# Loads of x split over two queues, regrouped 1x1 stores, an earlier branch, projection in image order and two blocks of logits together

## The chip, the cores and the metric

The kernel runs on one core of a Trainium2 chip. The metric is the device time of one execution in microseconds, the lower the better. The core has five engines with an instruction queue each: TensorE (PE) for matrix products, VectorE (DVE), ScalarE (ACT) and GpSimd (POOL) for elementwise work, and SyncE (SP), which here only issues DMAs. ACT and POOL can issue DMAs too. SBUF is the working memory, PSUM the memory that TensorE writes its products to, and HBM holds the inputs, the output and scratch arrays.

## The reference

The input x has 48 channels of 256 x 256. Two layers follow each other, each a residual on a group normalisation (16 groups, no learned scale):

```python
x = x + L0(gn(x))
x = x + L1(gn(x))

def L0(x):
    qkv = einsum('bchw,oc->bohw', x, w_qkv)          # 1x1, 48 -> 144
    qkv = dwconv3x3(qkv, w_dw)                       # depthwise
    q, k, v = split(qkv, 3)                          # each unfolded in 4x4 patches, padding 4
    q, k = l2norm(q), l2norm(k)                      # 8 heads of 96 channels
    attn = softmax(einsum('bhcn,bhcm->bhnm', q, k) * temperature)
    out = fold(einsum('bhcn,bhnm->bhcm', v, attn))   # sums over n
    return einsum('bchw,oc->bohw', out, w_proj)

def L1(x):                                           # in windows of 64 x 64, 3 terms
    return einsum('bcphqw,twW,thH,tcC->bCpHqW', xb, Ws, Hs, Cs)
```

There are 4096 patches inside the image (and a border of patches of zeros, which only adds to the sums of the softmax). Each head so makes a 4096 x 4096 matrix of exponentials.

## The kernel before

The image is cut into an upper and a lower half, which lie on partitions 16 to 63 and 64 to 111 (`rows_of`), so that 96 rows of partitions hold 48 channels twice.

**Start.** Ten pieces of x (seven of 16 rows of each half, then 8, 4 and 4) are loaded into `xr`, two DMAs a piece, all on SP (L442). ACT clears the 16 unused partitions of each piece (`clear`, L120), and DVE takes statistics of it (`bn_stats`, L444). `group_stats` makes mean and inverse deviation, which are folded into the weights.

**1x1 product of heads 0 and 1.** Their 36 channels of q, k and v are computed from `xr` in 16 groups of rows (L497 to L519). TensorE writes a PSUM tile, ACT and DVE each evict half of it into one of four buffers `oi`, and four DMAs store it to the scratch `t1[0]`: for each of two column blocks of 64 partitions (`c`) and each half of the image (`s`) one DMA of 36 partitions, the upper half on SP, the lower on POOL. The other six heads' product is done later, in strips, between the blocks of the attention (class `Strip`).

**Depthwise convolution of head 0** (`depthwise_first`, L382). Rows of `t1[0]` are loaded as `pad`; half of the rows are convolved on TensorE with nine diagonal matrices `diag` (made by nine POOL products, L387), half on DVE. After the normalisation q, k and v are stored to the scratch `qkv[0]`, q and k each as a high and a low part (`oh`, `ol`).

**Branch** (L538). A block for large temperatures follows under `tc.If`: a second pass that finds the maxima of the logits. With these inputs it isn't taken. Every engine loads the flag and jumps.

**Attention** (L572 to L801). The order of all engines is written out by hand (`tc.manual_schedule`). For each head and each of 32 blocks of 128 patches, `scores` makes the logits in four steps `j` of six products (L361), each followed by an exponential on ACT that also sums (L617). `normalised` divides v by the sum; `weigh` (L651) multiplies v with the exponentials of two blocks, and DVE adds the result to `oacc` (L665). PSUM tiles `big` have three buffers, exponentials `e` three. Before it, keys of head 0 are loaded over SP, ACT and POOL. The next head's convolution, its loads and stores and the strips are spread over the blocks. Results go to the scratch `os_`.

**Projection** (L803 to L902). The output of the attention is read back in eight parts, as `pot` tiles of 16 planes (one for each place in a 4 x 4 patch). The first part was loaded into four freed key tiles (`kt`). For each row `ki` of the patch, `project` multiplies with the weights into a PSUM tile that is ordered by plane (L818), and DVE adds it to x with a reading and writing order that steps by four pixels (L825); statistics for the second layer follow (L827), and POOL stores the result to `x1s` (L830). SP loads `pot` (L889) and x (L894); ACT clears the unused partitions of the tiles (L868 to L870).

**Layer 1** (L930 to L1083) contracts over channels, width and height on TensorE and is not touched.

Of the kernel before, what the change touches and what calls it, by code (L numbers as in the profile page):

```python
# [9 lines left out]
F32 = mybir.dt.float32  # L10
F32R = mybir.dt.float32r
AF = mybir.ActivationFunctionType
# [6 lines left out]
H = W = 256  # L19
HALF = H // 2  # L20
P2 = 2 * C
OFF = 16
# [27 lines left out]
def conv_preact_kernel(  # L50
# [114 lines left out]
    def both_halves(t, y, n, base=0):  # L165

        return [t[:, base + s * HALF + y : base + s * HALF + y + n, :] for s in range(2)]
# [9 lines left out]
    class Strip:  # L177
# [5 lines left out]
        def load(self):  # L183
            self.xs = xss[self.j % len(xss)]
            for s, rows in enumerate(both_halves(xc, SR * self.j, SR)):
                nc.sync.dma_start(out=self.xs[rows_of[s]], in_=rows)
# [21 lines left out]
        def store(self):  # L208
            for s, rows in enumerate(both_halves(t1[1], SR * self.j, SR, base=1)):
                nc.sync.dma_start(out=rows, in_=self.ot[:, s])  # L210
# [171 lines left out]
    def depthwise_first():  # L382

        with tc.tile_pool(name="dg", bufs=1) as dg, tc.tile_pool(name="dps", bufs=3, space=PSUM) as dps:
            diag = dg.tile([NP1, 9, NP1], F32, name="diag")
            for t in range(9):
                nc.gpsimd.tensor_scalar_mul(diag[:, t, :], ident[:NP1, :NP1], dwt[:, 0, t : t + 1])  # L387
# [3 lines left out]
            def taps(r):  # L391
# [12 lines left out]
            with tc.manual_schedule(engines={mybir.EngineType.PE}):  # L404
                taps(0)
                for i in range(0, CR + 1, 2):
                    if i + 1 not in on_tensor:
                        taps(i + 1)
                    taps(min(i + 2, CR))
# [17 lines left out]
    with tc.tile_pool(name="xn", bufs=1) as xnp, tc.tile_pool(name="cst", bufs=1) as cst, tc.tile_pool(  # L427
        name="nps", bufs=2, space=PSUM
# [64 lines left out]
        ois = [xnp.tile([128, 2, OR, W + 2], F32, name=f"oi{i}") for i in range(4)]  # L493
# [3 lines left out]
        for n in range(QR // OR):  # L497
# [32 lines left out]
    for t in ots:  # L530
        nc.gpsimd.memset(t[:, :, :, 0:1], 0.0)
        nc.gpsimd.memset(t[:, :, :, W + 1 : W + 2], 0.0)
    xss = [cv.tile([PF, SR, W], F32, name=f"xs{i}") for i in range(2)]
    for t in xss:
        nc.gpsimd.memset(t[:OFF], 0.0)
    depthwise_first()

    with tc.If(nc.values_load(large) > 0):  # L538
        with tc.tile_pool(name="sps", bufs=2, space=PSUM) as sps:
            for j in range(HALF // SR):  # L540
                w = Strip(j)
                w.load()
                w.run(sps)
                w.store()
        for h in range(1, NH):
            depthwise_all(h)
        with tc.tile_pool(name="mk", bufs=NM) as mk, tc.tile_pool(name="mq", bufs=2) as mq, tc.tile_pool(
            name="mps", bufs=2, space=PSUM
        ) as mps:
            for h in range(NH):  # L550
# [5 lines left out]
                for nb in range(NB):  # L556
# [13 lines left out]
                    nc.vector.tensor_reduce(nmx[:, b : b + 1], mx, AX.X, ALU.max, negate=True)  # L570

    with tc.tile_pool(name="ahead", bufs=2) as ah, tc.tile_pool(name="ae", bufs=3) as ae, tc.tile_pool(  # L572
# [34 lines left out]
        def scores(h, nb, behind=None):  # L607

            b = h * NB + nb
            e = ae.tile([128, NT], F32, name="e")  # L610
            zs = asm.tile([128, 5], F32, name="zs")
            nc.scalar.activation(zs[:, 4:5], nmx[:, b : b + 1], AF.Exp, bias=border)
            kts = [keys[h, m] for m in range(NM)]
            for j in range(4):
                ps = big.tile([128, 2, 512], F32, name="big")
                logits(ps, queries[h, nb // 2], kts, nb % 2 * 128, j)
                nc.scalar.activation(  # L617
                    e[:, j * 1024 : (j + 1) * 1024],
                    ps.rearrange("p a b -> p (a b)"),
                    AF.Exp,  # L620
                    bias=nmx[:, b : b + 1],
                    accum_out=zs[:, j : j + 1],
                )
                if j == 0 and behind:
                    behind()
            return h, nb, e, zs
# [73 lines left out]
        strips[0].load()  # L700
        with tc.manual_schedule():
            load_query(0, 1)
            block = scores(0, 0)
            for h in range(NH):
                more = h + 1 < NH
                rows = {r: Depthwise(h + 1, r) for r in range(CR + 1)} if more else {}
                for g in range(NG):
# [25 lines left out]
                    block = scores(h, g * G + 1, p and p.norm)  # L733
# [14 lines left out]
                    second = block  # L748
                    if g + 1 < NG:
                        block = scores(h, (g + 1) * G)  # L750
                    elif more:
                        block = scores(h + 1, 0)
                    blocks.append(normalised(*second))
# [22 lines left out]
                    for k in range(NK):  # L776
# [18 lines left out]
                        if not more and 0 < g <= 2 * NX and k in (1, 3):  # L795
                            i = (g - 1) * 2 + k // 2
                            t, y = i // 4, i % 4 * (RP // 4)
                            for half, src in enumerate(both_parts(xc, t, y, RP // 4)):
                                nc.sync.dma_start(out=xts[t][rows_of[half], y : y + RP // 4, :], in_=src)
# [9 lines left out]
        def project(k, pot, part, xt, new):  # L809

            R = xt.shape[1]
            n = R // KS * PX
            xv = xt.rearrange("p (py ki) (px kj) -> p ki kj py px", ki=KS, kj=KS)
            for ki in range(KS):
                ps = new(n)
                step = 512 // n
                for i in range(0, KS, step):
                    nc.tensor.matmul(  # L818
                        ps[:, i : i + step, :],
                        lhsT=wp,  # L820
                        rhs=pot(ki)[:PF, i : i + step, part * n : (part + 1) * n],
                        start=True,
                        stop=True,
                    )
                nc.vector.tensor_add(xv[:, ki], ps.rearrange("p k (py px) -> p k py px", py=R // KS), xv[:, ki])  # L825
# [3 lines left out]
            for half, rows in enumerate(both_parts(x1s, k, part * R, R)):  # L829
                nc.gpsimd.dma_start(out=rows, in_=xt[rows_of[half]])  # L830

        def in_big(n):

            ps = big.tile([128, 2, 512], F32, name="big")
            return ps[:PF].rearrange("p a (b n) -> p (a b) n", n=n)
# [26 lines left out]
    with tc.tile_pool(name="pj", bufs=1) as pj, tc.tile_pool(name="pjs", bufs=1) as pjs, tc.tile_pool(  # L862
# [3 lines left out]
        pxts = [pj.tile([PF, r, W], F32, name=f"pxt{t}") for t, r in enumerate((RP, RP, PR))]  # L866
# [19 lines left out]
        for k, xus_k in enumerate(xus, 1):  # L886
# [3 lines left out]
            if k >= NX:  # L890
                for part, xt in enumerate(xus_k):
                    R = xt.shape[1]
                    for s, rows in enumerate(both_parts(xc, k, part * R, R)):
                        nc.sync.dma_start(out=xt[rows_of[s]], in_=rows)  # L894
            for part, xt in enumerate(xus_k):
# [5 lines left out]
                    lambda n: pps.tile([PF, KS, n], F32, name="pps"),  # L901
# [223 lines left out]
```

## Time and profile before

| | us |
|---|---|
| runs: median of 3 (lowest to highest) | 3571.19 (3565.88 to 3576.49) |
| the profiled execution | 3563.74 |
| its span, first to last instruction | 3561.9 |
| TensorE busy | 3324.8 |
| granted TensorE clock, mean | 0.978 |
| exponentials on ACT (L617), 1024 times 1118 ns | 1144.6 |
| adds in the projection (L825), 1024 columns, first four | 1.98 each |
| adds of the attention (L665), 1024 columns | 1.22 each |

By time: x and its statistics until 88 us; the 1x1 product until 158; the convolution of head 0 until 281; loads of keys until 306; attention until 3188; projection and second statistics until 3324; layer 1 to the end.

In a group's row stand the line, engine and operation, output and input, how often, busy time, mean duration, and the idle time of the engine before it with what ended it. A window's row gives the busy time of each engine in a stretch, the clock granted to TensorE (1.00 is full), the share of time in which the 16 DMA engines were busy, and the bytes moved per second. The chain of waits follows the last instruction back through whatever released each step.

### The profile page before, as it was taken

To read this page: it belongs to the slowest core of one execution; us is meant where nothing else is said; L and a number is where in the kernel's file an instruction comes from. 1 tells how busy PE (TensorE), PEld (TensorE's weight loads), DVE (VectorE), ACT (ScalarE), POOL (GpSimd) and SP (SyncE) were. 2 spreads that over 40 slices of the span, in tenths; PEclk is the share of its full clock that TensorE was granted. 3 is DMA by queue.
4 is the path that set the end of the run, shared out by engine and by line. 5 is a ranking of instruction groups with operands and counts; after the bars stand their busy time and mean duration, and the time that the engine had idled before them with its cause. 6 is when DMAs were issued, how large, how long until landed. Compare 5 with 4: busy or idle time off the path is not lost.

```text
span 3561.9 us, 63455 instructions
## 1 busy us (share of the span) xinstructions
PE 3324.8 (93%) x25964; PEld 1856.3 (52%) x25964; DVE 1982.3 (56%) x2965; ACT 1953.2 (55%) x2891; POOL 588.0 (17%) x658
## 2 busy tenths in 40 slices
PE   0696999999999999999999999999999999986898
PEld 0243445555555555555555555555555555542576
DVE  4372666148825882588258826872687222228544
ACT  3234667657755665566557655764666444423243
POOL 2231111012211220122012201220122010000123
PEclk9897999999999999999999999999999999997999
DMA  9445666543332333333333332333333222109764
GB/s 147 143 127 147 164 161 165 168 137 93 86 87 79 93 87 83 89 95 82 85 87 95 79 87 83 93 89 78 87 96 93 76 53 51 33 25 295 176 163 112
DMA packets 232563, 380.22 MB, mean 107 GB/s; under 512 B 77858, under 2 KB 176546, under 8 KB 229192
## 3 DMA queue, kind: packets, MB, share of 16 engines
q1 hardware_dynamic: 192246, 262.98, 27.6%
q0 software_dynamic: 36544, 110.12, 13.7%
q8 instruction: 208, 3.41, 0.4%
q10 hardware_dynamic: 3474, 2.97, 0.3%
q14 instruction: 91, 0.75, 0.1%
HBM read 230.82 MB, written 144.90 MB: 105 GB/s over the span
## 4 chain that ended last, share of the span: by engine, by line
PE 85%; DMA 5%; DVE 1%; issue 1%; SPq 0%; ACT 0%; POOL 0%; POOLq 0%; DVEq 0%; ACTq 0%
PE big L361 39%; PE big L651 36%; PE pb L1015 2%; PE pa L991 2%; PE pc L1034 2%; DMA lxq<-in_x_dram 2%; PE big L194 2%; DMA xs<-in_x_dram 2%; PE pst L599 1%; DMA kt<-qkv 0%; PE pn L268 0%; PE pps L818 0%; DVE acc L249 0%; PE big L818 0%; DMA pad<-t 0%
## 5 line engine op out<-in xcount | busy, mean ns | idle before, releaser
L617 ACT ACTIVATE e<-big,nmx 128x1024 f32<-128x1024 f32 x1024 | 1144.6, 1118 | 909.6 <-PE big L361 883.7
L361 PE MATMUL big<-kt,qt 128*128 128x512 f32 x6144 | 1459.9, 395 | 29.7 <-DMA qt<-qkv 23.4
L651 PE MATMUL big<-e,vn 128*32 128x512 f32 x12288 | 1348.4, 593 | 1.0 <-DVE vn L635 1.0
L361 PEld LDWEIGHTS big<-kt,qt 128*128 128x128 f32 x6144 | 1143.3, 189 | 370.0 <-issue 122.0
L665 DVE TENSOR_TENSOR oacc<-big,oacc 128x1024 f32<-128x1024 f32 x359 | 438.5, 1221 | 766.9 <-PE big L651 766.9
L651 PEld LDWEIGHTS big<-e,vn 128*32 128x32 f32 x12288 | 384.5, 110 | 881.9 <-issue 815.5
L249 DVE SCALAR_TENSOR_TENSOR acc<-pad,dwt,acc 126x1024 f32<-126x1024 f32 x592 | 765.5, 1293 | 34.0 <-ACT acc L230 18.3
L319 POOL DMA_DIRECT2D qkv<-o x72 | 52.9, 734 | 1341.0 <-ACT o L303 1341.0
L313 POOL TENSOR_TENSOR ol<-o,oh 126x1024 fp32r<-126x1024 f32 x78 | 185.3, 2376 | 266.5 <-DVE ss L264 197.4
L631 DVE TENSOR_REDUCE zt<-zs 128x1 f32<-128x5 f32 x256 | 38.6, 151 | 327.6 <-ACT e L617 291.2
L617 ACT ACTIVATION_READ_ACCUMULATOR e<-big,nmx 128x1 f32 x1024 | 195.8, 191 | 0.0
L303 ACT COPY o<-acc 126x1024 f32<-126x1024 f32 x74 | 161.8, 2186 | 0.0
L1022 ACT COPY lyt<-pb 128x1024 f32<-128x1024 f32 x69 | 69.9, 1012 | 111.6 <-PE pb L1015 111.6
L201 ACT ACTIVATE ot<-big,bias 108x1024 f32<-108x1024 f32 x64 | 68.0, 1112 | 112.2 <-PE big L194 74.9
L230 ACT ACTIVATE acc<-pad,dwt 126x1024 f32<-126x1024 f32 x74 | 84.1, 1136 | 77.8 <-DMA pad<-t 69.7
L676 POOL DMA_DIRECT2D os__70<-oacc x86 | 50.3, 593 | 424.2 <-DVE oacc L665 414.4
L238 PE MATMUL dps<-pad,diag 126*126 126x512 f32 x216 | 95.6, 602 | 19.3 <-DMA pad<-t 19.3
L260 ACT ACTIVATE sq<-acc 126x1024 f32<-126x1024 f32 x74 | 78.2, 1057 | 59.6 <-DVE acc L249 48.5
L335 POOL DMA_DIRECT2D kt<-qkv x44 | 22.9, 538 | 516.6 <-PE big L361 418.9
L818 PE MATMUL pps<-pot,wp 112*112 112x512 f32 x112 | 68.9, 775 | 39.0 <-DMA pot<-os__70 20.7
L1001 DVE COPY lzt<-pa 128x864 f32<-128x864 f32 (+1 forms) x69 | 67.5, 1000 | 59.9 <-PE pa L991 59.9
L264 DVE TENSOR_REDUCE ss<-sq 126x64 f32<-126x1024 f32 x80 | 97.3, 1218 | 5.4 <-ACT sq L260 5.3
(154 smaller groups left out, 1973.4 us busy)
## 6 DMA issues: line engine op xcount, KB each, us to landing
pad<-t SPq DMA_DIRECT2D x238, 254.0 KB
t<-ot SPq DMA_DIRECT2D x64, 435.4 KB
qkv<-ol POOLq DMA_DIRECT2D x78, 336.0 KB, 6.4
qkv<-oh POOLq DMA_DIRECT2D x70, 336.0 KB, 5.7
qt<-qkv SPq DMA_DIRECT2D x176, 96.0 KB
xs<-in_x_dram SPq DMA_DIRECT2D x64, 192.0 KB
out_dram<-lrt POOLq DMA_DIRECT2D x96, 128.0 KB, 3.5
qkv<-o POOLq DMA_DIRECT2D x72, 168.0 KB, 3.4
```

The lines of the kernel that those rows point to most:

```text
L194: nc.tensor.matmul(ps[:M1, s, :], lhsT=wr[r], rhs=self.xs[r, i : i + 2, :].rearrange("p a b -> p (a b)"), start=True, stop=True,)
L230: nc.scalar.mul(self.acc, self.pad[:, 0:KS, 0:W], dwt[:, self.h, 0:1])
L238: nc.tensor.matmul(ps[:, i, :], lhsT=diag[:, tap, :], rhs=self.pad[:, y : y + 2, dx : dx + W], start=(tap == 0), stop=(tap == 8),)
L249: nc.vector.scalar_tensor_tensor(self.acc, self.pad[:, dy : dy + KS, dx : dx + W], dwt[:, self.h, tap : tap + 1], self.acc, ALU.mult, ALU.add,
L260: nc.scalar.activation(self.sq, self.acc, AF.Square)
L264: nc.vector.tensor_reduce(self.ss, self.sq.rearrange("p a (x b) -> p x a b", b=KS), AX.XY, ALU.add)
L303: nc.scalar.copy(self.o.rearrange("p (a b) x -> p a b x", a=KS), self.acc.rearrange("p a (x b) -> p a b x", b=KS))
L313: eng.tensor_sub(self.ol, self.o, self.oh.bitcast(F32))
L361: nc.tensor.matmul(ps[:, i, :], lhsT=qt[:, r, q0 : q0 + 128], rhs=kts[2 * j + i][:, r // 2, :], start=(r == 0), stop=(r == 2),)
L617: nc.scalar.activation(e[:, j * 1024 : (j + 1) * 1024], ps.rearrange("p a b -> p (a b)"), AF.Exp, bias=nmx[:, b : b + 1], accum_out=zs[:, ...
L651: nc.tensor.matmul(ps[p * 32 : (p + 1) * 32, u, :], lhsT=vn[:, c * 32 : (c + 1) * 32], rhs=e[:, n * 512 : (n + 1) * 512], start=(i == 0), ...
L665: nc.vector.tensor_add(oaccs[h, pair], ps, old)
```

## The change

1. `begin` issues the two halves of a transfer on the queues that it is given. The first load of x and the x loads of the projection go half on SP, half on ACT; on ACT the first ones are issued ahead of the clear of the same piece.
2. The 1x1 stores take both halves of the image in one DMA, and are split by partitions into 32 and 4; column block 0 goes to SP, block 1 to POOL. The buffers `oi` become five and get a pool of their own.
3. The branch stands behind the 1x1 product, ahead of the depthwise convolution of head 0; its block now does all eight heads. The `diag` products move to the start of the program, and the clearing of edges of `ot` and `xs` into a function that is called in the block and behind it.
4. `project` writes PSUM in image order (step of four columns within a bank), and the add is contiguous. The tiles `pxt` get a pool of their own ahead of `pot`.
5. `scores` takes several blocks and interleaves them by `j`; the first two blocks of head 0 are made together. The first strip's load is issued behind the second query's.

```diff
+    taps = ExitStack()
+    diag = taps.enter_context(tc.tile_pool(name="diag", bufs=1)).tile([NP1, 9, NP1], F32, name="diag")
+    for t in range(9):
+        nc.gpsimd.tensor_scalar_mul(diag[:, t, :], ident[:NP1, :NP1], dwt[:, 0, t : t + 1])
...
+    def begin(to, rows, engs, into=True):
+
+        for s in range(2):
+            a, b = (to[rows_of[s]], rows[s])
+            engs[s % len(engs)].dma_start(out=a if into else b, in_=b if into else a)
...
+            begin(xr[:, j : j + LR, :], both_halves(xc, j, LR), (nc.sync, nc.scalar))
             clear(xr[:, j : j + LR, :])
-            for s, rows in enumerate(both_halves(xc, j, LR)):
-                nc.sync.dma_start(out=xr[rows_of[s], j : j + LR, :], in_=rows)
...
-        ois = [xnp.tile([128, 2, OR, W + 2], F32, name=f"oi{i}") for i in range(4)]
+        ois = [oip.tile([128, 2, OR, W + 2], F32, name=f"oi{i}") for i in range(5)]
...
             for c in range(2):
-                for s, rows in enumerate(both_halves(t1[0], c * QR + n * OR, OR, base=1)):
-                    (nc.gpsimd if s else nc.sync).dma_start(out=rows, in_=ot[c * 64 : c * 64 + M0, s])
+                to = t1[0][:, 1 : H + 1, :].rearrange("c (s y) x -> c s y x", s=2)
+                to = to[:, :, c * QR + n * OR : c * QR + (n + 1) * OR, :]
+                for a, b in ((0, 32), (32, M0)):
+                    (nc.gpsimd if c else nc.sync).dma_start(out=to[a:b], in_=ot[c * 64 + a : c * 64 + b])
...
-    depthwise_first()
 
     with tc.If(nc.values_load(large) > 0):
+        edges()
...
-        for h in range(1, NH):
+        for h in range(NH):
             depthwise_all(h)
...
+    edges()
+    depthwise_first()
+    taps.close()
...
             for j in range(4):
-                ps = big.tile([128, 2, 512], F32, name="big")
-                logits(ps, queries[h, nb // 2], kts, nb % 2 * 128, j)
...
+                for h, nb, e, zs in blocks:
+                    b = h * NB + nb
+                    ps = big.tile([128, 2, 512], F32, name="big")
+                    logits(ps, queries[h, nb // 2], kts, nb % 2 * 128, j)
...
-        strips[0].load()
         with tc.manual_schedule():
             load_query(0, 1)
-            block = scores(0, 0)
+            strips[0].load()
+            block, other = scores(0, 0, 1)
...
             for ki in range(KS):
-                ps = new(n)
-                step = 512 // n
-                for i in range(0, KS, step):
+                ps = new(PY)
+                for y in range(0, PY, 2):
                     nc.tensor.matmul(
-                        ps[:, i : i + step, :],
+                        ps[:, y : y + 2, :].rearrange("p py (px kj) -> p kj py px", kj=KS),
                         lhsT=wp,
-                        rhs=pot(ki)[:PF, i : i + step, part * n : (part + 1) * n],
+                        rhs=pot(ki)[:PF, :, (part * PY + y) * PX : (part * PY + y + 2) * PX],
                         start=True,
                         stop=True,
                     )
-                nc.vector.tensor_add(xv[:, ki], ps.rearrange("p k (py px) -> p k py px", py=R // KS), xv[:, ki])
+                nc.vector.tensor_add(xv[:, ki], ps, xv[:, ki])
...
-        pxts = [pj.tile([PF, r, W], F32, name=f"pxt{t}") for t, r in enumerate((RP, RP, PR))]
+        pxts = [pjx.tile([PF, r, W], F32, name=f"pxt{t}") for t, r in enumerate((RP, RP, PR))]
...
-                    for s, rows in enumerate(both_parts(xc, k, part * R, R)):
-                        nc.sync.dma_start(out=xt[rows_of[s]], in_=rows)
+                    begin(xt, both_parts(xc, k, part * R, R), (nc.sync, nc.scalar))
```

More of the change, by code (lines that the diff above doesn't have):

```diff
@@ L162, in group_stats, with both_halves @@
         nc.vector.reciprocal(rstd, g)
-    def both_halves(t, y, n, base=0):
-        return [t[:, base + s * HALF + y : base + s * HALF + y + n, :] for s in range(2)]
+    def both_halves(t, y, n):
+        return [t[:, s * HALF + y : s * HALF + y + n, :] for s in range(2)]
+    def begin(to, rows, engs, into=True):
+        for s in range(2):
+            a, b = (to[rows_of[s]], rows[s])
+            engs[s % len(engs)].dma_start(out=a if into else b, in_=b if into else a)
     order = [(3, 0), (3, 1), (2, 0), (2, 1), (1, 1), (1, 0), (0, 1), (0, 0)]
@@ L184, in load @@
             self.xs = xss[self.j % len(xss)]
-            for s, rows in enumerate(both_halves(xc, SR * self.j, SR)):
-                nc.sync.dma_start(out=self.xs[rows_of[s]], in_=rows)
+            begin(self.xs, both_halves(xc, SR * self.j, SR), (nc.sync,))
         def run(self, pool):
@@ L208, in store @@
         def store(self):
-            for s, rows in enumerate(both_halves(t1[1], SR * self.j, SR, base=1)):
+            for s, rows in enumerate(both_halves(t1[1][:, 1:, :], SR * self.j, SR)):
                 nc.sync.dma_start(out=rows, in_=self.ot[:, s])
@@ L384, in depthwise_first, with on_row @@
         with tc.tile_pool(name="dg", bufs=1) as dg, tc.tile_pool(name="dps", bufs=3, space=PSUM) as dps:
-            diag = dg.tile([NP1, 9, NP1], F32, name="diag")
-            for t in range(9):
-                nc.gpsimd.tensor_scalar_mul(diag[:, t, :], ident[:NP1, :NP1], dwt[:, 0, t : t + 1])
             rows = [Depthwise(0, r, dg) for r in range(CR + 1)]
             on_tensor = [r for r in range(CR + 1) if r % 2 == 0 or r == CR]
-            def taps(r):
+            def on_row(r):
                 if r in on_tensor:
@@ L404, in depthwise_first @@
             with tc.manual_schedule(engines={mybir.EngineType.PE}):
-                taps(0)
+                on_row(0)
                 for i in range(0, CR + 1, 2):
                     if i + 1 not in on_tensor:
-                        taps(i + 1)
-                    taps(min(i + 2, CR))
+                        on_row(i + 1)
+                    on_row(min(i + 2, CR))
                     for d in rows[i + 6 : i + 8]:
@@ L427, in conv_preact_kernel @@
     with tc.tile_pool(name="xn", bufs=1) as xnp, tc.tile_pool(name="cst", bufs=1) as cst, tc.tile_pool(
+        name="oip", bufs=1
+    ) as oip, tc.tile_pool(
         name="nps", bufs=2, space=PSUM
@@ L529, in conv_preact_kernel, with edges @@
     ots = [cv.tile([M1, 2, SR, W + 2], F32, name=f"ot{i}") for i in range(NOT)]
-    for t in ots:
-        nc.gpsimd.memset(t[:, :, :, 0:1], 0.0)
-        nc.gpsimd.memset(t[:, :, :, W + 1 : W + 2], 0.0)
     xss = [cv.tile([PF, SR, W], F32, name=f"xs{i}") for i in range(2)]
-    for t in xss:
-        nc.gpsimd.memset(t[:OFF], 0.0)
-    depthwise_first()
+    def edges():
+        for t in ots:
+            nc.gpsimd.memset(t[:, :, :, 0:1], 0.0)
+            nc.gpsimd.memset(t[:, :, :, W + 1 : W + 2], 0.0)
+        for t in xss:
+            nc.gpsimd.memset(t[:OFF], 0.0)
     with tc.If(nc.values_load(large) > 0):
+        edges()
         with tc.tile_pool(name="sps", bufs=2, space=PSUM) as sps:
@@ L605, in conv_preact_kernel, with scores @@
         nc.vector.memset(border, math.log(NBORDER))
[L607 to L612, printed above, removed]
+        def scores(h, *nbs, behind=None):
+            blocks = []
+            for nb in nbs:
+                b = h * NB + nb
+                e = ae.tile([128, NT], F32, name="e")
+                zs = asm.tile([128, 5], F32, name="zs")
+                nc.scalar.activation(zs[:, 4:5], nmx[:, b : b + 1], AF.Exp, bias=border)
+                blocks.append((h, nb, e, zs))
             kts = [keys[h, m] for m in range(NM)]
             for j in range(4):
-                ps = big.tile([128, 2, 512], F32, name="big")
-                logits(ps, queries[h, nb // 2], kts, nb % 2 * 128, j)
[L617 to L623, printed above, removed]
+                for h, nb, e, zs in blocks:
+                    b = h * NB + nb
+                    ps = big.tile([128, 2, 512], F32, name="big")
+                    logits(ps, queries[h, nb // 2], kts, nb % 2 * 128, j)
+                    nc.scalar.activation(
+                        e[:, j * 1024 : (j + 1) * 1024],
+                        ps.rearrange("p a b -> p (a b)"),
+                        AF.Exp,
+                        bias=nmx[:, b : b + 1],
+                        accum_out=zs[:, j : j + 1],
+                    )
                 if j == 0 and behind:
                     behind()
-            return h, nb, e, zs
+            return blocks
         def normalised(h, nb, e, zs):
@@ L732, in conv_preact_kernel @@
                     blocks = [normalised(*block)]
-                    block = scores(h, g * G + 1, p and p.norm)
+                    if h or g:
+                        (other,) = scores(h, g * G + 1, behind=p and p.norm)
                     if p:
@@ L747, in conv_preact_kernel @@
                             d.tap(t)
-                    second = block
                     if g + 1 < NG:
-                        block = scores(h, (g + 1) * G)
+                        (block,) = scores(h, (g + 1) * G)
                     elif more:
-                        block = scores(h + 1, 0)
-                    blocks.append(normalised(*second))
+                        (block,) = scores(h + 1, 0)
+                    blocks.append(normalised(*other))
                     if d:
@@ L797, in conv_preact_kernel @@
                             t, y = i // 4, i % 4 * (RP // 4)
-                            for half, src in enumerate(both_parts(xc, t, y, RP // 4)):
-                                nc.sync.dma_start(out=xts[t][rows_of[half], y : y + RP // 4, :], in_=src)
+                            begin(xts[t][:, y : y + RP // 4, :], both_parts(xc, t, y, RP // 4), (nc.sync,))
                         if not more and 2 * NX < g <= 2 * NX + KS and k in (1, 3):
@@ L811, in project @@
             R = xt.shape[1]
-            n = R // KS * PX
-            xv = xt.rearrange("p (py ki) (px kj) -> p ki kj py px", ki=KS, kj=KS)
+            PY = R // KS
+            xv = xt.rearrange("p (py ki) x -> p ki py x", ki=KS)
             for ki in range(KS):
-                ps = new(n)
-                step = 512 // n
-                for i in range(0, KS, step):
+                ps = new(PY)
+                for y in range(0, PY, 2):
                     nc.tensor.matmul(
-                        ps[:, i : i + step, :],
+                        ps[:, y : y + 2, :].rearrange("p py (px kj) -> p kj py px", kj=KS),
                         lhsT=wp,
-                        rhs=pot(ki)[:PF, i : i + step, part * n : (part + 1) * n],
+                        rhs=pot(ki)[:PF, :, (part * PY + y) * PX : (part * PY + y + 2) * PX],
                         start=True,
@@ L828, in project @@
                 seen.append(i)
-            for half, rows in enumerate(both_parts(x1s, k, part * R, R)):
-                nc.gpsimd.dma_start(out=rows, in_=xt[rows_of[half]])
+            begin(xt, both_parts(x1s, k, part * R, R), (nc.gpsimd,), into=False)
         def in_big(n):
             ps = big.tile([128, 2, 512], F32, name="big")
-            return ps[:PF].rearrange("p a (b n) -> p (a b) n", n=n)
+            return ps[:PF].rearrange("p a (b x) -> p (a b) x", x=W)
         with tc.manual_schedule():
@@ L860, in load_piece @@
         eng.dma_start(out=piece(yw, i)[rows_of[s], y : y + n, :], in_=x1s[:, y0 : y0 + n, :])
-    with tc.tile_pool(name="pj", bufs=1) as pj, tc.tile_pool(name="pjs", bufs=1) as pjs, tc.tile_pool(
+    with tc.tile_pool(name="pjx", bufs=1) as pjx, tc.tile_pool(name="pj", bufs=1) as pj, tc.tile_pool(name="pjs", bufs=1) as pjs, tc.tile_pool(
         name="pps", bufs=3, space=PSUM
@@ L900, in conv_preact_kernel @@
                     xt,
-                    lambda n: pps.tile([PF, KS, n], F32, name="pps"),
+                    lambda n: pps.tile([PF, n, W], F32, name="pps"),
                 )
```

## The prediction

> **What bounds the kernel now.** I read the page first: its busy shares, its forty slices and the chain that ended last, then busy time by window to see where TensorE is not full.
>
> ```profile
> PE 3324.8 (93%) x25964; PEld 1856.3 (52%) x25964; DVE 1982.3 (56%) x2965; ACT 1953.2 (55%) x2891; POOL 588.0 (17%) x658
> ...
> PE   0696999999999999999999999999999999986898
> ...
> PE 85%; DMA 5%; DVE 1%; issue 1%; SPq 0%; ACT 0%; POOL 0%; POOLq 0%; DVEq 0%; ACTq 0%
> ```
>
> TensorE is the bound from about 310 us to 3188 us, where the slices read 9 throughout. Two products make 75% of the chain, L361 39% and L651 36%; the change touches neither, but for the order of the first 48 products. So everything happens in the first 310 us and between 3190 and 3320 us. The windows of those two ends (columns: length, busy PE, weight loads, DVE, ACT, POOL, granted clock, DMA share, GB/s):
>
> ```profile
> 2.00:20.00 18.00, 0.00 (x0) 0.00 (x0) 7.12 (x24) 17.99 (x7) 5.41 (x10) 1.00 1.03 148
> 20.00:40.00 20.00, 0.00 (x0) 0.00 (x0) 8.48 (x15) 11.63 (x6) 2.72 (x6) 1.00 1.00 143
> ...
> 82.00:86.00 4.00, 0.00 (x0) 0.00 (x0) 4.00 (x8) 0.00 (x0) 2.21 (x4) 1.00 0.89 216
> 107.00:154.00 47.00, 30.99 (x226) 8.68 (x224) 19.26 (x16) 16.32 (x15) 16.07 (x32) 0.85 0.64 199
> ...
> 3192.00:3206.00 14.00, 10.00 (x16) 3.73 (x16) 5.79 (x3) 0.25 (x1) 0.22 (x1) 0.66 0.06 16
> 3206.00:3225.00 19.00, 9.49 (x15) 3.87 (x16) 11.31 (x13) 19.00 (x6) 1.04 (x2) 0.64 0.99 308
> 3225.00:3235.00 10.00, 6.18 (x14) 2.02 (x12) 9.97 (x11) 8.81 (x2) 1.03 (x2) 1.00 1.04 183
> ```
>
> The load of x (to 88 us) is DMA at a share of 1.0, yet only 145 GB/s. The stores of the 1x1 product (107 to 158 us) hold a share of 0.64. In the projection the DMAs stand still for 14 us (share 0.06) and are then full until 3310 us. The chain there says the same: after the first projection it waits on loads, 9.65 us for pot and 29.82 and 33.54 us for x.
>
> ```profile
> 3195.59 10.02 PE big L818 x16
> 3205.60 0.05 issue
> 3205.65 0.07 POOL csn L872
> 3205.73 9.65 DMA pot<-os__70
> 3215.38 0.14 issue
> ...
> 3239.48 29.82 DMA lxq<-in_x_dram
> 3269.32 33.54 DMA lxq<-in_x_dram
> ```
>
> **The change part by part.** All sums are against the profiled execution, 3563.7 us (span 3561.9). The median of the runs shown is 3571.2, 7.5 us more, so I subtract the same gain from it.
>
> **x on two queues** (20 loads, 10 moved to ACT). SP issued all 20 at 0.31 us each, 6 us in all, long before the data came, so issue time is hidden and removing it is worth nothing. On ACT each issue now stands ahead of a clear (3.6 us each, 28 us in all); the clears end near 34 us instead of 30, with the load running until 88. Does a second queue add bandwidth? The queue rows of the first 83 us:
>
> ```profile
> q1 hardware_dynamic: 1166, 12.26, 97.2%
> q0 software_dynamic: 1019, 0.15, 3.1%
> ```
>
> The packets of the one queue already fill 97.2% of 16 engines. With two queues busy (3240 to 3250 us) the shares were 56.6% and 45.2%, again 101.8% together: an engine serves one packet at a time. The Trainium skill, "DMA: Bandwidth & Descriptors", section "Issuing engines are not separate DMA queues", says the same as a rule, that starting DMAs from several engines saves only issue time. Rule and row give 0 us. Against both stands that these packets are slow: 145 GB/s here, but 216 from 82 to 86 us, when the last pieces of 8 and 4 rows come. If mixing the halves did what smaller rows do, 12.58 MB at 216 GB/s would take 58 us in place of 83, 25 us less. Statistics (64 x 0.676 = 43 us of DVE) would still hide. Bounds: +2 to -25; I take 0, by the queue row.
>
> **Stores of 32 and 4 rows, five buffers.** Before, each group of rows sends 4 DMAs of 36 partitions, 16 groups in 47 us, 2.9 us a group. Evictions without a wait came 1.72 us apart (107.45, 109.16, 110.88 us), so the stores set the pace. A share of 0.64 is 10.2 engines at a time. By the skill's same page (how many engines a DMA uses) 36 partitions spread over 12 engines, 32 over 16 and 4 over 4; 10.2 of 12 would be 85% full. Packets on the busiest engine per group: 12 before (four times 3); after, 4 + 4 from the two large stores, 2 from the small store on SP's queue, about 0.5 from POOL's, 10.5. So 2.9 x 10.5/12 = 2.54 us a group: 16 x 0.36 = **6 us** saved. From below 0 (small DMAs cost as much as they spare), from above 16 x (2.9 - 1.72) = 19 us. The number of DMAs stays 64. The fifth buffer can't add much: SP's store still waits for the one four groups back.
>
> **Branch behind the 1x1 product, diag early.** Before, SP ended its last store at 281.14, and the first key load started at 285.83 on ACT and 286.32 on SP. ACT had had nothing to do since 275.3, so its branch was long past; it still waited until 285.83, for the last store of `ol`, issued at 278.98 (POOL's like ones landed after 6.4 us). So the landing ends last, not the branch: removing it gives 0.5 us on SP. In its new place each engine waits for the t1 stores anyway (SP's last issue 153.6, pad load 158.35), about as long as the 4.6 us here: 0 to 3 us if the cover is short, I take 0. Diag's nine POOL products (5.3 us) move from 160 to about 87 us, where POOL is idle until 107; before they ended at 165.3, just ahead of the pads at 166.9, so nothing is won. Sum **0.5 us**.
>
> **First two blocks together.** Before, TensorE had done 14 of 72 products of the first three blocks by 305.9 us, and ACT's first exponential came at 305.68, since ACT issued key loads until then. The PSUM pool has three buffers, so TensorE can now do at most 18 by then; from there 12 exponentials at 1.3 us set the pace, the ninth ending at 317.4, and block 2's last logits at about 320 in place of 324.4. That is 4 us; the value loads land late in both, so I take **3 us** (0 to 5).
>
> **Projection.** (a) The pot tiles no longer share memory with the kt tiles that the first projection reads. The built order shows it: the pot1 load waits for an earlier TensorE product and the clears, and the three clears on ACT stand before the last stores. So pot loads start near 3194 in place of 3205.73. The DMAs have 104 us of full work there (3206 to 3310), so what starts 11.7 us earlier ends 11.7 us earlier. One clear (3.6 us) now stands before ACT's kt loads and delays the first projection by 0.7 us. (b) The adds become contiguous: 32 adds of 1024 columns' worth at 1.96 us fall to 1.22, the row of L665 (PSUM plus SBUF, 1024, contiguous): 23.7 us of DVE. But DVE stands beside full DMAs; I credit only the tail, 2 us. (c) Half of x goes behind ACT's clears: three pxt and the 8.73 us of lxq, 18 us from 3206, so pxt0's second half starts at 3224 in place of 3207. It is needed at its add, about 3230 to 3240: a stall of 0 to 8 us, which I leave at 0 because other loads and stores fill the DMAs meanwhile. (d) TensorE now writes PSUM at steps of 16 bytes. The Trainium skill, "PSUM — Partial Sum Buffer", section "Specifications (TRN2)", speaks against it: lines of 8 bytes, and any non-contiguous pattern slows matmuls significantly. No row here has such a write. The nearest: 48 products of L361 take 11.10 us, 231 ns for 512 contiguous columns, one 8-byte line per 0.90 ns. An fp32 record of L238 takes 32.89 us / 72 = 457 ns, 0.89 ns a column. At one line per column the strided fp32 write needs the line rate that L361 already shows. By the row 0 us; by the rule, if records double, 79 us of TensorE here become up to 158, in a stage of 118. I take 0. Sum 11.7 - 0.7 + 2 = **13 us**, from -30 to +28.
>
> **Sum:** 0 + 6 + 0.5 + 3 + 13 = 22.5 us. 3563.7 - 22.5 = 3541.2; from the median, 3571.2 - 22.5 = **3549 us**.
>
> **Rivals.**
> - *x really comes faster* (chance 0.27). For it: 216 GB/s with short rows, and in the projection single-queue x at 183 against about 310 with others mixed in. Against it: full engines. 25 us more: 3524.
> - *The pot head start is lost* (0.13), because the second halves of x, behind the clears, leave DVE waiting, or because x on both queues delays pots. Then 22.5 - 13 = 9.5 remain: 3562, no measurable change.
> - *Strided PSUM writes* (0.10), the slower case. It decides once a record at L837 passes 118 us / 128 = 0.92 us in that stage; at double price the stage grows by 40 us, less 9.5 of the other gains: about 3600.
> - *The forecast* (0.50), 3537 to 3560.
>
> About 0.3%, 10.7 us, is what a measurement of this kernel can tell from no change. Faster by more: nearly all of forecast and first rival, 0.78; within: 0.12; slower: 0.10. The range 3514 to 3575 leaves out most of the slower rival and the best end of the first.
>
> **What would show it.** x: statistics still ending near 88 us, two queues of some 49% each at 145 GB/s. Stores: 41 us in place of 47, share near 0.73. Keys still starting about 4.6 us after the last store's issue. Weights-times-values first at about 4 us sooner after the keys. Pot loads beginning before the first projection ends; adds at 1.22 us; TensorE records at L837 still near 0.6 to 0.8 us. The forecast is wrong if x's stage shortens by over 8 us, if L837's mean passes 0.92 us, or if the DMAs are idle again after 3208.

## The result and the profile after

| | before | after |
|---|---|---|
| runs: median (lowest to highest), us | 3570.02 (3563.62 to 3576.49), 5 runs | 3551.57 (3544.47 to 3557.27), 5 runs |
| ratio, 95% interval | | 0.995 [0.9928, 0.9971] |
| profiled execution, us | 3563.74 | 3557.27 |
| its span, us | 3561.9 | 3555.5 |

The change saves 18.45 us between medians; the interval reaches from 10 to 26 us. The profiled execution of the changed kernel is the longest of its five, so its trace shows only 6.5 us of this. The page of the changed kernel (busy time, TensorE's slices, shares of the chain):

```profile
PE 3314.1 (93%) x25964; PEld 1852.0 (52%) x25964; DVE 1958.1 (55%) x2965; ACT 1952.7 (55%) x2891; POOL 589.7 (17%) x660
...
PE   0596999999999999999999999999999999996898
...
PE 86%; DMA 5%; DVE 2%; SPq 1%; ACT 1%; issue 1%; ACTq 0%; POOL 0%; POOLq 0%; DVEq 0%
```

TensorE bounds the same middle as before. Its windows at the two ends, in the columns used before:

```profile
2.00:20.00 18.00, 0.00 (x0) 0.00 (x0) 7.23 (x24) 14.70 (x5) 4.93 (x10) 1.00 1.01 165
20.00:40.00 20.00, 0.00 (x0) 0.00 (x0) 9.81 (x17) 3.60 (x1) 2.62 (x5) 1.00 1.02 168
...
104.00:156.00 52.00, 28.26 (x228) 8.78 (x220) 19.25 (x15) 16.59 (x15) 17.77 (x32) 0.86 0.74 179
3196.00:3204.00 8.00, 6.37 (x8) 2.29 (x8) 1.40 (x2) 4.62 (x2) 0.00 (x0) 0.57 0.93 222
...
3240.00:3260.00 20.00, 3.13 (x4) 1.37 (x5) 4.41 (x5) 0.00 (x0) 0.00 (x0) 0.50 1.00 233
```

Three things differ from the forecast. The load of x moves 165 to 168 GB/s where it moved 143 to 148, at the same full engines. The 1x1 stores have busier engines (0.74 in place of 0.64), yet move fewer bytes per second (179 in place of 199). In the projection the pots do start early, at 3196, but from 3240 to 3260 full engines carry only 233 GB/s and DVE has 4.4 us of work. The chain there:

```profile
3196.99 8.41 DMA kt<-os__70
...
3229.47 26.14 DMA pot<-os__70
3255.61 3.47 DVE pxt L844 x3
...
3268.26 32.87 DMA pot<-os__70
```

The first projection waits 8.41 us more for its last key-tile loads, which ACT issues late (3194.95 to 3197.61) beside SP's pots. Then comes a wait of 26 us, ended by an add into `pxt`.

One trace of each kernel is not enough here: the attention, which no kernel of this study alters but for its first blocks, took between 2853.9 and 2874.6 us in 14 traces. So I compare the same stage over all traces that share its code. From the start instants of instructions in the traces, in us, mean (range; number of traces):

| stage | as before | as changed | difference |
|---|---|---|---|
| statistics of x begin their sum | 89.0 (85.1 to 94.2; 6) | 83.2 (80.8 to 85.5; 4) | -5.8 |
| first 1x1 store to first depthwise product | 59.5 (57.6 to 61.5; 7) | 66.2 (66.1, 66.4; 2) | +6.8 |
| first depthwise product to first key load | 119.6 (118.9 to 120.2; 7) | 118.6 (117.6 to 119.7; 7) | -1.0 |
| first key load to first weights-values product | 36.1 (35.3 to 38.5; 8) | 34.2 (33.9 to 34.4; 6) | -1.9 |
| last such product to the second statistics' sum | 132.6 (128.8 to 135.7; 5) | 124.1 (121.8 to 125.3; 4) | -8.5 |

They sum to -10.4, the small end of the measured interval. In the same traces two stretches that no edit touches, the attention behind its first blocks and layer 1, were on average 3.0 and 3.4 us shorter in the changed kernel and the five built on it. Their ranges overlap those of the others, and nothing here shows a cause.

### The profile page after: what moved, and what is told of

Its sections match the earlier page's. It is cut to its first block, busy times and chain, and to the rows that moved or that the text cites. A ratio compares the mean times of both kernels' runs of the same rounds, so it can differ in the third digit from the quotient of the medians.

```text
span 3555.5 us, 63466 instructions
## 1 busy us (share of the span) xinstructions
PE 3314.1 (93%) x25964; PEld 1852.0 (52%) x25964; DVE 1958.1 (55%) x2965; ACT 1952.7 (55%) x2891; POOL 589.7 (17%) x660
## 3 DMA queue, kind: packets, MB, share of 16 engines
q0 software_dynamic: 36544, 110.12, 13.9%
## 4 chain that ended last, share of the span: by engine, by line
PE 86%; DMA 5%; DVE 2%; SPq 1%; ACT 1%; issue 1%; ACTq 0%; POOL 0%; POOLq 0%; DVEq 0%
PE big L370 39%; PE big L672 36%; PE pb L1032 2%; PE pa L1008 2%; DMA xs<-in_x_dram 2%; PE pc L1051 2%; DMA pot<-os__70 2%; PE big L203 2%; PE dps L247 1%; DVE acc L258 1%; PE pst L615 1%; SPq L344 0%; DVE st L846 0%; DMA kt<-qkv 0%; DMA pad<-t 0%
## 5 line engine op out<-in xcount | busy, mean ns | idle before, releaser
L370 PEld LDWEIGHTS big<-kt,qt 128*128 128x128 f32 x6144 | 1142.4, 189 | 367.1 <-issue 120.2
L258 DVE SCALAR_TENSOR_TENSOR acc<-pad,dwt,acc 126x1024 f32<-126x1024 f32 x592 | 765.5, 1293 | 34.4 <-ACT acc L239 18.7
L837 PE MATMUL pps<-pot,wp 112*112 112x512 f32 x112 | 60.9, 699 | 39.5 <-DVE pxt L844 22.6
```

The lines of the kernel that those rows point to most:

```text
L258: nc.vector.scalar_tensor_tensor(self.acc, self.pad[:, dy : dy + KS, dx : dx + W], dwt[:, self.h, tap : tap + 1], self.acc, ALU.mult, ALU.add,
L370: nc.tensor.matmul(ps[:, i, :], lhsT=qt[:, r, q0 : q0 + 128], rhs=kts[2 * j + i][:, r // 2, :], start=(r == 0), stop=(r == 2),)
```

## The experiments

Ratios are to the kernel before, run on the same chip.

**x alone.**

```diff
-                nc.sync.dma_start(out=xr[rows_of[s], j : j + LR, :], in_=rows)
+                (nc.scalar if s else nc.sync).dma_start(out=xr[rows_of[s], j : j + LR, :], in_=rows)
```

> The kernel before with one edit: the second half of each piece of x is loaded from ACT, ahead of ACT's clear of that piece. Theory 1 (two queues let the DMA engines move the same bytes faster, as the changed kernel's profile has it): the statistics' aggregate starts near 84.4 us in place of 88.2, the rate over the first 83 us is near 154 GB/s in place of 150, the time is 3 to 4 us less (ratio 0.999). Theory 2 (the prediction: the engines serve one packet at a time and are full with one queue): the aggregate at 88.2 within 0.5 us, time unchanged; the 3.8 us seen in the changed kernel were then chance or another edit's.

Measured: sum of the statistics at 82.26 us, ratio 0.9972 [0.9958, 0.9987], 10 us less (5 to 15). Theory 2, that of the prediction, falls. The queue rows of 2 to 60 us show how; first the kernel before, then the changed one (packets, MB, share of 16 engines):

```profile
q1 hardware_dynamic: 676, 8.44, 98.5%
```

```profile
q1 hardware_dynamic: 444, 5.42, 58.7%
q10 hardware_dynamic: 320, 3.93, 40.3%
```

The engines are as full as before, but 58 us of 16 engines, 928 engine-us, at 98.5% for 8.44 MB are 108 us a MB; with two queues 99.0% for 9.35 MB are 98. The same bytes took less of the engines' time. The share says that engines are occupied, not that they move bytes at their best rate.

**Shorter rows on one queue.**

```diff
-        parts = [16] * 7 + [8, 4, 4]
+        parts = [8] * 15 + [4, 4]
```

> The kernel before with one edit: x comes in 15 pieces of 8 rows and 2 of 4 in place of 7 of 16, one of 8 and 2 of 4, all from SP's one queue. So far two queues brought the statistics' aggregate to 80.8 to 84.4 us, one queue to 88.2 to 94.2. Theory 1 (a second queue is what helps): aggregate stays at 88 us or later, no change in time. Theory 2 (16 KB rows are slow and shorter ones are not, as the last pieces' 216 GB/s suggested): with 8 KB rows the rate of one queue rises to about 200 GB/s, the aggregate comes near 65 to 70 us, time 18 to 25 us less.

Measured: 75.53 us, ratio 0.9978 [0.9961, 0.9996], 8 us less (1 to 14). One queue of 2 to 60 us in this kernel:

```profile
q1 hardware_dynamic: 1626, 10.04, 98.9%
```

That is 91 engine-us a MB, without a second queue. Theory 2 has the direction, but not the size: 177 GB/s, not 200, and less than half of the forecast time. A single trace is not firm here: the kernel `best_1q` below has the same loads and needs 101 engine-us a MB. In the window of 2 to 60 us of all 14 traces, engine-us for a MB of x:

| | pieces of 16 rows | pieces of 8 rows |
|---|---|---|
| one queue | 102 to 115 (6 traces) | 91, 101 |
| two queues | 92 to 99 (4 traces) | 83, 86 |

So two means lower the price of a MB, the second queue for both sizes of piece. The load of x of the kernel before was full by its share and still not at the engines' limit. Why a MB costs less in these ways no run here shows.

**The stores alone, the form put back, all of it put back.**

```diff
-                for s, rows in enumerate(both_halves(t1[0], c * QR + n * OR, OR, base=1)):
-                    (nc.gpsimd if s else nc.sync).dma_start(out=rows, in_=ot[c * 64 : c * 64 + M0, s])
+                for a, b in ((0, 32), (32, M0)):
+                    (nc.gpsimd if c else nc.sync).dma_start(out=to[a:b], in_=ot[c * 64 + a : c * 64 + b])
```

> The kernel before with one edit: the stores of the 1x1 product go out as 32 and 4 channels of both halves, c picking the queue; still four buffers in the old place. Theory 1 (this form of store is itself slower): from SP's first of these stores to its last it takes about 52 us in place of 46.4, a DMA share near 0.75, the time is 5 to 7 us more (ratio 1.0015 to 1.002). Theory 2 (the form is faster, as predicted, and the slow stage of the changed kernel comes from the fifth buffer or the new place of the buffers): 41 us, time 5 to 6 us less. Theory 3 (the changed kernel's profile caught a slow stage by chance): 46 to 47 us, no change.

> The changed kernel with only the form of the 1x1 stores put back: 36 channels of one half in each DMA, the half picking the queue; five buffers in their own pool stay. Theory 1 (the form costs time): SP's stores take 46 us or less again, the first depthwise product starts near 163.5 us in place of 169.8, the time is some 6 us below the changed kernel (ratio to the kernel before near 0.993). Theory 2 (the fifth buffer or its place costs it): the stage stays near 52 us and the ratio at 0.995. Theory 3 (chance): stage 46, ratio 0.995, since the changed kernel's other runs had it too.

> The changed kernel with the 1x1 stores put back in full: form, queue by half, four buffers in the old place. With the form alone put back SP's stores took 48.3 us from first to last (44.0 to 44.9 in three kernels with the old form and four buffers, 52.3 in the changed kernel). Theory 1 (the fifth buffer or its place cost some 3.5 us, the form as much again): 44 to 45 us here, the first depthwise product 58 to 62 us after the first store. Theory 2 (what stands around the stage in the changed kernel, the early branch or the diag products, costs it): 48 us again. The time ratio to the kernel before near 0.993 in both.

SP's first to last 1x1 store took 45.8 us (44.0 to 47.5; 10 traces) with the old form and four buffers, 47.75 with the new form and four, 48.26 with the old form and five, 52.33 and 51.61 with both new. The form alone thus added less than theory 1 of its run said (52), putting the form back alone did not bring back 46, and with all put back it was 46.9. From the first store to the first depthwise product the stores alone took 60.35 us, inside the range of the old form (57.6 to 61.5). Ratios in the order of the runs: 1.0012 [0.9998, 1.0026], 0.9944 [0.9923, 0.9965], 0.9946 [0.9929, 0.9963]. The stage is longer in the changed kernel, and both the form and the fifth buffer seem to have a part; single traces for each do not settle the shares, and no time of these three separates from its neighbour. The stores' totals and queues, 107 to 152 us of the kernel before and 104 to 156 us of the changed one:

```profile
DMA packets 3381, 8.96 MB, mean 199 GB/s; under 512 B 1219, under 2 KB 1219, under 8 KB 3377
...
q0 software_dynamic: 1978, 4.56, 34.1%
q1 hardware_dynamic: 1399, 4.35, 30.0%
```

```profile
DMA packets 3430, 9.32 MB, mean 179 GB/s; under 512 B 1192, under 2 KB 1192, under 8 KB 3419
...
q0 software_dynamic: 2048, 4.76, 41.1%
q1 hardware_dynamic: 1371, 4.44, 32.0%
```

As many packets, but each costs more: 0.641 x 16 x 45 / 3377 = 137 ns before, 0.731 x 16 x 52 / 3419 = 178 ns after (174 in the stores-alone kernel, 140 with the old form and five buffers). Between the first and the last of these stores a packet took 174, 178 and 181 ns in the three traces with the new form, and 136 to 140 in the eleven with the old one. The dearer packet goes with the form, not with the buffers.

**The branch alone.** Branch, edges and `diag` as in the change, everything else as before.

> The kernel before with one edit: branch and edges' memsets ahead of the depthwise stage, diag products at the start. Theory 1 (the branch costs in its new place what the trace of the changed kernel shows, and gives little in the old one): from the first 1x1 store to the first depthwise product 62 to 63 us in place of 57.6 to 60.4, from there to the first key load 117.6 to 118.4 in place of 118.9 to 120.1; sum 1 to 3 us slower. Theory 2 (the predicted 0.5 us gain): both stretches as before or shorter, no change to be measured. The rival that the branch gates the keys would take 4 to 5 us from the second stretch.

Measured: 59.33 us to the first depthwise product, 118.43 from there to the keys, ratio 0.9988 [0.9971, 1.0005]. The first half of theory 1 falls: no cost of the branch shows in its new place. No change of the time can be told either. Beside the change's other edits, with the old stores, the first stretch took 61.3 us (60.9 to 61.9; three traces); whether the branch has a part in these 1.8 us is open. Over seven traces each, SP's last store of `ol` stands 5.9 us ahead of the first key load with the branch moved, 7.0 before: 1.2 us gained. The landing of that store still ends last.

**The projection alone, with and without ACT's half of x.** Image order and separate pools on the kernel before; in the first of the two also

```diff
-                    for s, rows in enumerate(both_parts(xc, k, part * R, R)):
-                        nc.sync.dma_start(out=xt[rows_of[s]], in_=rows)
+                    begin(xt, both_parts(xc, k, part * R, R), (nc.sync, nc.scalar))
```

> The kernel before with only the projection's edits: PSUM written in image order, x tiles in a pool of their own so that the pots no longer share memory with the key tiles, second halves of x from ACT. Theory 1 (what the changed kernel's profile shows: the pots start 9.4 us earlier, but get ahead of ACT's last loads for the first projection, so that this ends 5 us later): from the last product of the attention to layer 1's first rows 6 to 7 us less than before, layer 1 about 2 us less; time 6 to 9 us less (ratio near 0.998). Theory 2 (the predicted sum holds and the changed kernel's profiled run was a slow one): 13 us less in the projection, ratio 0.9963. Theory 3 (strided PSUM writes slow TensorE): products at L818's place above 0.92 us each, time more than before.

> The kernel before with the projection's image order and separate pools, but x from SP alone. With ACT's half of x the stage from the last product of weights and values to the aggregate took 124.2 to 125.3 us in three kernels, without any edit of it 130.5 to 134.7. Theory 1 (the halves on ACT behind its clears make DVE wait 20 us for pxt and so eat part of the head start): 119 to 121 us here, time ratio near 0.996. Theory 2 (the DMA engines are full either way and only the bytes count): 124 to 126 us. Theory 3 (as for the first load of x, two queues help): 127 us or more.

Measured: with ACT's half the stage took 124.22 us, ratio 0.9974 [0.9961, 0.9988]; with SP alone 118.19 us, 0.9947 [0.9929, 0.9966]. Each run comes nearest to its theory 1, though the clears that the second names are not what holds the halves back (below). Over the four traces of each kind (the three kernels of the better version also load x from SP alone) the stage took 124.1 us (121.8 to 125.3) with ACT's half and 118.7 (116.2 to 122.9) without it. So the second queue, a gain in the first load, is a loss here, 5.4 us by these means. In all four traces with ACT's half DVE stands idle for 20 to 21 us before its first add into `pxt`; in the four without it for 5 to 8. In the chain of the kernel with ACT's half the reason stands by name:

```profile
3211.15 19.72 DMA csn<-in_Cs_dram
3230.89 42.77 DMA pxt<-in_x_dram
```

`csn` (27 KB a DMA) is loaded by ACT just ahead of its halves of x. In the changed kernel's trace the order on ACT and the queues of 3212 to 3236 us (q1 is SP's, q0 POOL's, q10 ACT's) are:

```profile
3211.47 0.83 ACTq L892 DMA_DIRECT2D csn<-in_Cs_dram  x2
3212.33 0.92 ACTq L177 DMA_DIRECT2D pxt<-in_x_dram  x2
```

```profile
q1 hardware_dynamic: 310, 4.26, 62.7%
q0 software_dynamic: 240, 3.10, 37.1%
q10 hardware_dynamic: 278, 0.05, 1.6%
```

ACT's queue (q10) moves 278 packets of together 0.05 MB in 24 us, about one for each of the 310 that carry SP's 4.26 MB. ACT's 768 KB halves of x, issued at 3212.33, stand behind these crumbs: its first packets of 16 KB come only after 3236, and 89 of them, 1.46 MB, until 3256. The add into `pxt` needs both halves and so starts at 3255.61. (The changed kernel's chain above names `pot` for this wait. SP's half of `pxt` is not likely the last: up to its end SP's queue held 336 packets of 16 KB, the pots ahead included, and it moved 476 from 3196 to 3236.) Two windows in the same place of the stage, 20 us each, in the kernel with x from SP alone:

```profile
3232.00:3252.00 20.00, 10.83 (x16) 3.65 (x16) 12.22 (x17) 0.00 (x0) 1.03 (x2) 0.77 1.01 334
3252.00:3272.00 20.00, 10.49 (x17) 3.86 (x18) 12.92 (x21) 0.00 (x0) 3.09 (x6) 0.67 1.02 296
```

DVE works 12 us in 20 in place of 4.4, and the full engines move 334 and 296 GB/s in place of 233. That ACT's half makes DVE wait is shown by eight traces. A kernel with `csn` on another queue was not tried, so that `csn` is what holds it back is read from the queues and this chain.

**Image order alone.**

> The kernel before with one edit: the projection writes PSUM in image order (strided for TensorE, contiguous for DVE); pots still share memory with the key tiles, x from SP. Stage from the last product of weights and values to the aggregate: 128.8 to 135.7 us without any edit of the projection, 118.2 with this and the separate pools. Theory 1 (the prediction: the head start of the pots is worth most, the adds only the tail of 2 us): 130 us or so, time ratio 0.9990 to 0.9995. Theory 2 (shorter adds free the buffers earlier and so are worth as much as the pools): 123 to 126 us, ratio near 0.998. Products at 0.70 us each if strided writes cost nothing.

Measured: 128.83 us, ratio 0.9986 [0.9975, 0.9997], 5 us less (1 to 9). Theory 1 has the stage, if the ratio is a little better than it said. The stage itself shows no gain yet: 128.83 lies at the end of the range without the edit (128.8 to 135.7). The adds did become shorter, from 1.98 us; in the changed kernel, with the same order (min/median/max ns):

```profile
L844 DVE TENSOR_TENSOR xt<-pps,xt x8: 1205/1210/1212, 3216.9 to 3229.6; 112x1024 f32<-112x1024 f32 x8
```

TensorE's products of the later parts, min/median/max ns, in the kernel before and in the changed one:

```profile
L818 PE MATMUL pps<-pot,wp x112: 592/593/1195, 3215.5 to 3312.8; 112*112 112x512 f32 x112
```

```profile
L837 PE MATMUL pps<-pot,wp x112: 592/592/1196, 3212.4 to 3310.8; 112*112 112x512 f32 x112
```

Writing at a step of 16 bytes in PSUM cost these fp32 products nothing.

**A better version.** The changed kernel with x in pieces of 8 rows, the stores of before, and the projection's x on SP; the same with x on one queue; the same with the change's stores and two queues.

> The changed kernel with three parts replaced: x in pieces of 8 rows, still on two queues; the 1x1 stores as before the change; the projection's x on SP alone. Theory 1 (gains of the stages add): aggregate of the statistics near 70 us if the second queue still helps with short rows, near 75.5 if not; projection stage near 118 us in place of 125; in all 16 to 22 us below the changed kernel, ratio to the kernel before 0.989 to 0.991. Theory 2 (parts overlap or give back later): ratio 0.993 or above.

> As best_2q, but x in pieces of 8 rows from SP's queue alone. Theory 1 (what slows x is the 16 KB row of a piece, and two queues only mend part of that): aggregate near 75.5 us or earlier, the same as with two queues within the spread of 2 us. Theory 2 (a second queue helps whatever the rows): some 5 us later than best_2q.

> As best_2q, but with the change's own 1x1 stores (32 and 4 channels, five buffers). Theory 1 (they cost what the profiles show): from the first 1x1 store to the first depthwise product 64 to 66 us in place of 58 to 62, time 4 to 6 us above best_2q (ratio 0.0012 to 0.0017 higher). Theory 2 (the prediction): 6 us below it. Theory 3 (the stage varies that much from run to run): equal within 2 us.

| | sum of x | store to depthwise | projection stage | median, us | ratio |
|---|---|---|---|---|---|
| two queues | 74.53 | 60.94 | 117.51 | 3534.82 | 0.9919 [0.9903, 0.9935] |
| one queue | 82.90 | 60.99 | 116.15 | 3537.81 | 0.9925 [0.9910, 0.9940] |
| the change's stores | 77.20 | 66.40 | 122.91 | 3540.38 | 0.9929 [0.9912, 0.9945] |

The first is 29 us below the kernel before. By the ratios it is 11 us below the changed kernel, less than the 16 to 22 of its theory 1. Its interval lies below the changed kernel's ratio of 0.995 and overlaps the lower end of that ratio's own interval (from 0.9928). In its x load:

```profile
2.00:20.00 18.00, 0.00 (x0) 0.00 (x0) 10.42 (x30) 11.48 (x7) 7.53 (x14) 1.00 1.04 215
20.00:40.00 20.00, 0.00 (x0) 0.00 (x0) 9.09 (x15) 7.39 (x4) 5.09 (x10) 1.00 1.04 188
```

The stages of its trace, against the means of the table above: 14.5 gained on x, 1.5 lost up to the first depthwise product (with the stores of before), 1.5 gained to the keys, 1.8 on the first blocks and 15.1 on the projection. They make 31, near the 29 of the median; for the other two kernels the same sums give 23 against 26, and 17 against 24. The change's stores cost 5.5 us of their stage against the old ones in the same company, and 5.6 us of the median; the intervals of the ratios overlap, so the stage is shown and the time not. One queue against two can't be told apart by time. By the stage, x came 8.4 us later from one queue than from two here, as theory 2 of that run has it, but the earlier kernel with such loads from one queue was 7.4 us faster in it (75.53).

## Why the prediction was right in its total and wrong in its terms

It said 22.5 us; 18.45 were measured, well inside its range. The terms, by the stages of the table:

- **x on two queues**, predicted 0, came to -5.8. The failed step: "rule and row give 0 us". The row was the 97.2% of one queue, read as a limit. The page of the Trainium skill on "DMA: Bandwidth & Descriptors" ("Issuing engines are not separate DMA queues") agreed with this reading, and the run with x alone contradicts both: SP's issues cost 6 us in all and were hidden, and the whole kernel gained 10 us (5 to 15). The argument against, 216 GB/s with short rows, was in the text and was the better one. The rival built on it had the direction; its 25 us were four times too large.
- **Stores**, predicted -6, came to +6.8, or +5 against the old stores beside the same other edits (61.3 us, three traces). The failed step: the count of packets on the busiest engine (10.5 for 12) took the price of a packet as fixed. With the 178 ns that they then cost in place of 137, the same sum gives 10.5 x 178/137 = 13.6, 2.9 x 13.6/12 = 3.3 us a group, and 16 x 0.4 = 6 us more. This repair is no proof: for the stores alone, at 174 ns, it gives 5 us more, and SP's stretch grew by 2. Why the packets grew dearer is not settled. (The share of 0.64 in the sum is that of 107 to 154 us; up to 158 it is 0.60.)
- **Branch**, predicted -0.5 with no cost in the new place: -1.0 and none. Right, and so was the reason, the landing that ends last. `diag` was moved in the same run, and no gain or loss from it shows.
- **First two blocks**, predicted -3, came to -1.9: right in kind. The first exponential still waits on ACT's key loads. No run has this edit alone.
- **Projection**, predicted -13, came to -8.5. Parts (a) and (b) held as a sum: with x from SP alone the stage took 118.7 us against 132.6, a gain of 13.9. The image order alone gave 5 us of the time (1 to 9), which holds the 2 credited. Part (c), "a stall of 0 to 8 us, which I leave at 0", is the failed step: it costs 5.4 us. The reason given there, that other transfers fill the DMAs meanwhile, held for the share (1.00) and not for the bytes (233 GB/s in place of 296 to 334). The place named was wrong too: ACT issued the first half 1.25 us after SP's, so it waited in the queue, by its packets behind `csn`, and not behind the clears. The rival that loses the pot head start thus came true in part.
- **Strided PSUM**: the row of L361 was the right one to argue from. The rule on "PSUM — Partial Sum Buffer" in the Trainium skill (section "Specifications (TRN2)"), that non-contiguous patterns slow products significantly, doesn't hold for this fp32 write (592 ns against 593).

That the total came close was in part luck. The times of the runs with one part each make -10 (x), -9 (projection), +4 (stores) and -4 (branch) us, together -19, each to about 5 us either way, and the last two are not clear of 0. Against the forecast's 0, -13, -6 and -0.5 the gain on x stands in for the loss in the stores and in part (c). The stages tell it less evenly: there the losses outweigh x, and their sum is 10.4 us. The total alone would have confirmed a sum of which one large term had the wrong sign and two others, x and part (c), were missing.

## What to carry to other kernels

A DMA share near 1.0 says that the engines hold packets, not that they move bytes at their best rate: compute engine time per MB or per packet, and compare it with other windows of the same trace before calling a transfer bound. Here spreading a load over a second queue helped where that queue was empty, and cost time where small packets stood ahead in it; look first at what is queued there, however few bytes that is. Where an edit regroups DMAs, do not reuse the price of a packet from the old grouping.

## What was not expected of the hardware

- With the engines full, a MB of x took 102 to 115 engine-us from one queue and 92 to 99 from two; in pieces of 8 rows in place of 16 it took 91 and 101 from one, 83 and 86 from two.
- Two queues seem to take turns by packet, whatever its size: 278 packets of 0.05 MB took as long as 310 of 4.26 MB beside them.
- The 1x1 stores moved 179 GB/s at a DMA share of 0.74 and 199 GB/s at 0.64.
